# A two-layer graph network: which nodes are summed by counting and which by gathering, and how a float is split into three bf16 words

## The chip, the cores and the metric

The kernel runs on one core of one Trainium2 chip. The metric is the device time of one execution in microseconds (us), taken over several runs of the same program. One execution is also recorded by the profiler; its span runs from the first to the last instruction. The engines are called by the names of the profile: PE is TensorE (matrix products; PEld its weight loads), DVE is VectorE, ACT is ScalarE, POOL is GpSimd, SP is SyncE, which here only issues transfers.

## The reference

There are 12500 nodes with 256 features each and 200000 edges, sorted by destination. Destinations are skewed: `dst` is 12500 times the square of a uniform number, so low-numbered nodes receive many edges and high-numbered ones few. Two layers of mean aggregation are followed by a linear layer, a residual and a layer norm:

```python
def _sage_conv(x, src, dst, W_l, b_l, W_r):
    msgs = x[src]
    agg = jax.ops.segment_sum(msgs, dst, num_segments=N_NODES)
    deg = jax.ops.segment_sum(jnp.ones((src.shape[0],), x.dtype), dst, num_segments=N_NODES)
    mean = agg / jnp.maximum(deg, 1.0)[:, None]
    return mean @ W_l + b_l + x @ W_r

h = jax.nn.relu(_sage_conv(x, src, dst, W1_l, b1, W1_r))
h = jax.nn.relu(_sage_conv(h, src, dst, W2_l, b2, W2_r))
x = _layernorm(x + h @ W3 + b3, axis=-1)
```

All of it is float32.

## The kernel before

**Two ways to sum.** A segment sum is made in one of two ways. For the *cold* nodes (many nodes, few edges each) POOL gathers the rows of 128 source nodes at a time from DRAM with an indirect transfer (L251). A round is four such gathers. PE then multiplies the gathered rows by a 0/1 selection matrix (L263), which DVE makes by a comparison (L208), and the partial sums are placed by a second selection (L214, L279) and added by DVE into a ring of node blocks in SBUF (L293). There are four buffers `got`, so POOL can be some rounds ahead of PE.

For the *hot* nodes (few nodes, very many edges) nothing is gathered. Nodes are taken in groups of `DN` = 256. For a group the kernel first makes a matrix of counts: how many edges lead from each source node to each of the 256 nodes (`count`, L665). A tile of 128 edges is turned into 0/1 matrices by DVE (`pick` L680, `low` L684, `aft` L690), multiplied by PE into PSUM (L723, L727), and copied by ACT at a running offset into `counts` (L729). Then the sum is a dense product of counts and the whole node table (`product`, L642). The table is stored as three bf16 words per float, so that the product is exact: 98 blocks of source nodes times 3 words times 2 halves are 588 matmuls per group (L655), fed by 49 loads `rows` of 384 KB (L649) into four buffers.

**The words.** `split_rows` (L636) makes the three bf16 words of x in `x3_d` for layer 1, and `first_block` (L907) those of h in `h3_d` for layer 2. Both call `exact` (L629), in which ACT rounds the float to bf16, DVE subtracts it, ACT rounds the rest, and DVE subtracts again.

**Which groups are where.** `HG1` groups are summed by counts in layer 1 and `HG` in layer 2 (L102). The gathers of a layer begin behind its hot groups, at edge tile `lows[HG1]` or `lows[HG]`. Layer 1 runs in stages (`stages_1`, L807): in stage 0 group 0 is counted and x is split; in stage g group g is counted while the product of group g-1 runs, its degrees are summed (L744), and its counts are stored in DRAM (`stored`, L776). Two count buffers alternate. Groups 0 to 3 are stored; group 4 is kept and group 5 is counted already, so that layer 2 can begin with them. Layer 2 (`stages_2`, L819) takes groups 4, 5, 6, 0, 1, 2, 3 in this order: group 6 is counted during the product of group 5, and the stored counts of groups 0 to 3 are loaded again (`loaded`, L781) one stage ahead of their products.

**What orders the work.** PE and POOL keep the order in which the program is written; DVE, ACT and SP are ordered by the framework's scheduler. `layer` (L576) goes through the rounds of gathers. In each it issues the four gathers of the next round, the products of this round, pieces of finished node blocks (`first_block` or `last_block`), and as much dense and counting work as is due. What is due is a straight line: the planner's cost of all stages (`cost_of`) times the share of rounds done, reaching the whole eight rounds before the end (L615). Within a stage `mixed` (L762) takes its parts in proportion to their costs. So the counting and dense work is spread evenly over the rounds, and a change in the number of stages or rounds changes how much of it stands in each.

Before the gathers of layer 2 can start, all rows of h must have been written. The code that runs in case the edges do not fit the expected law (`by_sorting`) is not executed here.

Of the kernel before, what the change touches and what calls it, by code (L numbers as in the profile page):

```python
# [7 lines left out]
F32 = mybir.dt.float32  # L8
F16 = mybir.dt.float16
BF16 = mybir.dt.bfloat16  # L10
# [3 lines left out]
OP = mybir.AluOpType  # L14
# [9 lines left out]
P = 128  # L24
# [3 lines left out]
def kernel(tc, x, src, dst, w1l, b1, w1r, w2l, b2, w2r, w3, b3, out):  # L28

    args = (x, src, dst, w1l, b1, w1r, w2l, b2, w2r, w3, b3, out)
    flag = tc.nc.dram_tensor("unfit_d", (1, 1), I32).ap()
    by_runs(tc, *args, flag)
    with tc.tile_pool(name="flag", bufs=1) as pool:
        unfit_i = pool.tile([1, 1], I32, name="unfit_i")  # L40
        tc.nc.sync.dma_start(unfit_i, flag)
        unfit = tc.nc.values_load(
            unfit_i[0:1, 0:1], min_val=0, max_val=1,
            skip_runtime_bounds_check_because="it is clamped to 0..1 where it is made")
    with tc.If(unfit > 0):
        by_sorting(tc, *args)
# [3 lines left out]
def by_runs(  # L50
# [27 lines left out]
    nc = tc.nc  # L78
    N, D = x.shape
    E = src.shape[0]  # L80
    NB = -(-N // P)
# [15 lines left out]
    def at_most(t):  # L97
        return N * ((t + SLACK) / NT) ** 2 + 2

    HG1, HG, DN = 5, 7, 256  # L102
    lows = [max(t for t in range(0, NT, 2 * G) if t == 0 or at_most(t) < DN * g) for g in range(HG + 1)]
    highs = [min(t for t in range(0, NT, G) if at_least(t) >= DN * (g + 1)) for g in range(HG)]
    HT = highs[-1]
# [189 lines left out]
    with tc.tile_pool(name="setup", bufs=1) as su, \  # L295
# [172 lines left out]
        for g, (c0, c1) in enumerate(spans):  # L468
            n = c1 - c0
# [46 lines left out]
        for t in range(0, HT, 32):  # L516
            n = min(32, HT - t)
# [52 lines left out]
    work = ctx.enter_context(tc.tile_pool(name="work", bufs=2))  # L570
# [57 lines left out]

    def exact(t, s, rest):  # L629

        nc.scalar.copy(s[:, 0], t)
        nc.vector.tensor_tensor(rest, t, s[:, 0], op=OP.subtract)
        nc.scalar.copy(s[:, 1], rest)
        nc.vector.tensor_tensor(s[:, 2], rest, s[:, 1], op=OP.subtract)

    def split_rows(b):  # L636
        t = load_rows(x, N, b, "split_sb")
        s = work.tile([P, 3, D], BF16, name="parts")
        exact(t, s, t)
        nc.sync.dma_start(x3_d[:, b], s)  # L640

    def product(g, table3, c_sb):  # L642
# [116 lines left out]
    def counting(g):  # L759
        return sum(count_cost(t) for t in range(lows[g], highs[g]))  # L760
# [20 lines left out]
    def loaded(g, c_sb):  # L781
        for b0 in range(0, NB, 14):
            nc.sync.dma_start(c_sb[:, b0:b0 + 14, :DN], count_d[g, :, b0:b0 + 14])
            yield 0.5

    def dense(g, table3, c_sb, waiting, with_deg):
        for p in product(g, table3, c_sb):
            if isinstance(p, float):
                yield p
            else:  # L790
                d_sb = p
        if with_deg:
            yield from degrees(g, c_sb)
        for j in range(DN // P):
            waiting.append((g * (DN // P) + j, d_sb[:, :, j * P:(j + 1) * P]))

    def splits():
        for b in range(NB):
            split_rows(b)
            yield COST_SPLIT  # L800
# [1 line left out]
    D_1 = NB * COST_DENSE + DN // P * (NB // 14) * COST_DEGREES  # L802
    D_2 = NB * COST_DENSE
    MOVED = NB // 14 * 0.5
    assert NB % 14 == 0 and HG == HG1 + 2

    def stages_1(waiting):  # L807

# [9 lines left out]

    def stages_2(waiting):  # L819

        order = [HG1 - 1, HG1, HG1 + 1, *range(HG1 - 1)]
        for i, g in enumerate(order):
            parts = [(dense(g, h3_d, counts[(HG1 - 1 + i) % 2], waiting, False), D_2)]
            if 1 <= i < HG - 1:
                n = order[i + 1]
                to = counts[(HG1 + i) % 2]
                parts.append((count(n, to), counting(n)) if n > HG1 else (loaded(n, to), MOVED))
            yield parts
# [15 lines left out]
    def load_rows(table, n_rows, b, name, tag=None):  # L844
        t = work.tile([P, D], F32, name=name, tag=tag or name)
        n = min(P, n_rows - b * P)
        if n < P:
            nc.vector.memset(t, 0.0)
        nc.sync.dma_start(t[:n], table[b * P:b * P + n, :])
        return t  # L850
# [56 lines left out]
    def first_block(b, agg=None):  # L907
        x_sb = load_rows(x, N, b, "x_sb")
        of_ring = agg is None
        if of_ring:  # L910
            overlap(b, True)
            agg, deg_row = ring(b)
            nc.sync.dma_start(deg_d[b:b + 1], deg_row)
        yield True
        if of_ring:
            deg = work.tile([P, 1], F32, name="deg")
            with nc.allow_non_contiguous_dma(reason="a row becomes a column"):
                nc.sync.dma_start(deg, deg_d[b, :, None])
        x_t, copied = transposed(x_sb, turned(), "own_t")
        yield True  # L920
        if of_ring:
            nc.vector.tensor_scalar(deg, deg, 1.0, None, op0=OP.max)
            nc.vector.reciprocal(rdeg[:, b:b + 1], deg)
        h, own = sage(x_t, copied, b, agg, of_ring, w1l_sb, w1r_sb, biases[:, 0], "h")
        if of_ring:
            nc.scalar.copy(deg_row, zeros[0:1, 0])
        nc.sync.dma_start(h_d[b * P:(b + 1) * P, :], h)
        s = work.tile([P, 3, D], BF16, name="parts")
        exact(h, s, own)
        nc.sync.dma_start(h3_d[:, b], s)  # L930
        yield True
# [37 lines left out]
    block_pool = ctx.enter_context(tc.tile_pool(name="block_ps", bufs=2, space=PSUM))  # L969
    count_pool = ctx.enter_context(tc.tile_pool(name="count_ps", bufs=1, space=PSUM))  # L970
    layer(Gathers(h_d, True), last_block, 5, staged(stages_2), cost_of(stages_2))


# [377 lines left out]
```

## Time and profile before

| what | value |
|---|---|
| time, median of 3 runs | 2878.88 us (2876.56 to 2884.81) |
| the profiled execution | 2859.28 us, its span 2857.5 us |
| mean granted clock of TensorE | 0.918 |
| PE busy, matmul instructions | 2325.8 us (81%), 18268 |
| DVE busy | 1461.6 us (51%) |
| ACT busy | 1099.4 us (38%) |
| POOL busy, instructions | 2054.2 us (72%), 2074 |
| gathers in layer 1, in layer 2 | 1076 at 1031 ns, 988 at 954 ns |
| transfers | 676.49 MB, mean 237 GB/s |

Times are microseconds unless marked ns. A row of the groups gives line, engine and operation, output and inputs with their shapes, the number of instructions, the busy time and the mean ns of one, and the idle time before them with what ended it. "issue" is idle time in which the engine waited for nothing that the profile shows. A row of waits names the waiting group, what released it, the total, the number of times and the longest. A row by stretches gives the stretch, its length, the busy time of PE, PEld, DVE, ACT and POOL with instruction counts, the granted clock, the busy share of the transfer engines and GB/s. Matmuls overlap in PE, so the busy time of a group is less than its count times its mean.

### The profile page before, as it was taken

The numbers are of one execution on the slowest core, as the hardware profiler recorded it, in microseconds if no ns is written. First come the engines' busy times: TensorE is split into PE (matmuls) and PEld (weight loads), VectorE is DVE, ScalarE is ACT, GpSimd is POOL, SyncE is SP. The second block draws the span as 40 slices with busy tenths as digits, with TensorE's granted clock in tenths as the row PEclk, the third lists the DMA queues.
The fourth block names the chain that finished last, engine by engine and source line by source line (L and its number), as shares of the span: only waits on it lengthen the run. The fifth ranks groups of instructions, "written<-read, shape, count | busy, mean of one in ns | idle before, by whom it ended". The sixth has DMA issues, their size and how long they took to land.

```text
span 2857.5 us, 53445 instructions
## 1 busy us (share of the span) xinstructions
PE 2325.8 (81%) x18268; PEld 1607.4 (56%) x18268; DVE 1461.6 (51%) x4334; ACT 1099.4 (38%) x2270; POOL 2054.2 (72%) x2074
## 2 busy tenths in 40 slices
PE   3466675888988998999996678777889889999995
PEld 1122333565755666766664455555656667777773
DVE  6688774654555565565564124443324344444443
ACT  0422774654554564565563013333112122222222
POOL 5777775677777777777675777777777777777771
PEclk9876877997998999999997999999999999999998
DMA  4466679778878879877764777777989999888872
GB/s 124 135 180 179 190 210 300 248 225 257 267 224 254 291 219 297 262 215 228 247 212 132 229 244 231 222 225 226 294 285 306 295 301 309 283 264 270 271 248 70
DMA packets 420975, 676.49 MB, mean 237 GB/s; under 512 B 72420, under 2 KB 279386, under 8 KB 420698
## 3 DMA queue, kind: packets, MB, share of 16 engines
q1 hardware_dynamic: 316263, 400.60, 43.5%
q0 software_dynamic: 99072, 270.66, 31.3%
q8 instruction: 150, 2.46, 0.4%
q10 hardware_dynamic: 5362, 1.72, 0.3%
q14 instruction: 128, 1.04, 0.1%
HBM read 582.84 MB, written 89.92 MB: 235 GB/s over the span
## 4 chain that ended last, share of the span: by engine, by line
PE 45%; DMA 24%; POOL 11%; issue 8%; DVE 7%; ACT 4%; SPq 1%; DVEq 0%; ACTq 0%; POOLq 0%
PE dense_ps L655 17%; POOL got L251 11%; PE part_ps L263 6%; PE block_ps L878 5%; DMA got<-h_d,src_t 4%; DMA rows<-h_d 4%; PE block_ps L883 4%; PE count_ps L723 4%; DMA x_sb<-in_x_dram 4%; PE sum_ps L279 4%; DMA rows<-x_d 4%; DMA split_sb<-in_x_dram 3%; DMA got<-in_x_dram,src_t 2%; PE block_ps L950 2%; PE block_ps L855 2%
## 5 line engine op out<-in xcount | busy, mean ns | idle before, releaser
L251 POOL DMA_INDIRECT got<-in_x_dram,src_t x1076 | 1109.7, 1031 | 420.3 <-issue 282.7
L251 POOL DMA_INDIRECT got<-h_d,src_t x988 | 942.4, 954 | 329.4 <-issue 260.8
L655 PE MATMUL dense_ps<-counts,rows 128*128 128x256 bf16 x7056 | 958.4, 279 | 75.4 <-DMA rows<-h_d 41.1
L655 PEld LDWEIGHTS <-rows 128*128 128x128 bf16 x7056 | 674.2, 99 | 296.7 <-issue 81.4
L729 ACT CAST counts<-count_ps 128x686 f32 (+2 forms) x620 | 540.2, 872 | 237.8 <-PE count_ps L723 188.0
L263 PE MATMUL part_ps<-got,one 128*32 128x257 f32 (+1 forms) x4128 | 359.9, 422 | 181.9 <-DMA got<-h_d,src_t 106.1
L723 PE MATMUL count_ps<-pick,low 128*128 128x490 bf16 (+2 forms) x1052 | 321.1, 359 | 62.5 <-ACT counts L729 37.2
L680 DVE TENSOR_SCALAR pick<-steps,key_t 128x686 bf16<-128x686 f16 (+2 forms) x748 | 301.0, 414 | 120.9 <-PE count_ps L723 107.3
L208 DVE TENSOR_TENSOR one<-lo_t,lane_b 128x128 f32<-128x128 bf16 x516 | 148.1, 287 | 322.5 <-PE part_ps L263 318.8
L273 ACT COPY some<-part_ps 128x257 f32<-128x257 f32 (+1 forms) x361 | 134.5, 373 | 414.2 <-PE part_ps L263 413.1
L279 PE MATMUL sum_ps<-two,some 128*128 128x128 f32 x1444 | 240.9, 293 | 39.4 <-DVE own L890 38.6
L263 PEld LDWEIGHTS part_ps<-got,one 128*32 128x32 f32 x4128 | 87.2, 112 | 299.8 <-issue 237.9
L279 PEld LDWEIGHTS sum_ps<-two,some 128*128 128x128 f32 x1444 | 209.4, 205 | 55.3 <-DVE own L890 39.9
L293 DVE TENSOR_TENSOR sums<-sums,sum_ps 128x256 f32 x361 | 148.3, 411 | 145.8 <-PE sum_ps L279 113.2
L886 ACT COPY sums<-zero 128x256 f32<-128x256 f32 x172 | 69.3, 403 | 393.4 <-PE block_ps L883 391.8
L889 DVE TENSOR_TENSOR own<-block_ps,biases 128x256 f32<-128x256 f32 x196 | 82.6, 421 | 210.3 <-PE block_ps L883 209.9
L723 PEld LDWEIGHTS <-low 128*128 128x128 bf16 x1052 | 105.0, 101 | 140.0 <-DVE pick L680 33.6
L857 ACT COPY own_t<-block_ps 128x256 f32<-128x256 f32 x294 | 108.8, 372 | 125.6 <-PE block_ps L855 124.5
L684 DVE TENSOR_TENSOR low<-low_t,lane_b 128x512 bf16<-128x512 bf16 x187 | 127.7, 683 | 39.4 <-PE count_ps L727 39.0
L892 ACT ACTIVATE h<-own 128x256 f32<-128x256 f32 x196 | 81.7, 417 | 145.3 <-DVE own L890 145.0
L727 PE MATMUL count_ps<-aft,low 128*128 128x98 bf16 x614 | 133.3, 217 | 0.0
L878 PE MATMUL block_ps<-w1l_sb,sums 128*128 128x256 f32 x352 | 114.2, 453 | 12.5 <-DVE sums L293 6.0
(177 smaller groups left out, 2417.9 us busy)
## 6 DMA issues: line engine op xcount, KB each, us to landing
rows<-h_d SPq DMA_DIRECT2D x343, 384.0 KB
rows<-x_d SPq DMA_DIRECT2D x245, 384.0 KB
count_d<-counts SPq DMA_DIRECT2D x28, 896.0 KB
counts<-count_d SPq DMA_DIRECT2D x28, 896.0 KB
x_sb<-in_x_dram SPq DMA_DIRECT2D x194, 128.0 KB
x_d<-parts SPq DMA_DIRECT2D x98, 192.0 KB
h_d<-parts SPq DMA_DIRECT2D x98, 192.0 KB
got<-in_x_dram,src_t POOLq DMA_INDIRECT x1076
```

The costliest lines, as they stand in the source:

```text
L208: nc.vector.tensor_tensor(one, lo[:, a:a + n * (G - 1) + 1:n].unsqueeze(2).to_broadcast([P, G, W]), lane_b[:, :W].unsqueeze(1).to_broadcas ...
L251: rows = nc.gpsimd.indirect_dma_start(out=g[:, j, :D], out_offset=None, in_=self.table, in_offset=bass.IndirectOffsetOnAxis(ap=src_t[:, e: ...
L263: strip = nc.tensor.matmul(part_ps[j * W:(j + 1) * W, :width], lhsT=one[:, j], rhs=g[:, j, :width], start=r == 0, stop=r == n - 1)
L273: nc.scalar.copy(some[:, :width], part_ps[:, :width])
L279: nc.tensor.matmul(sum_ps[:, c], lhsT=some[:, c * P:(c + 1) * P], rhs=two, start=True, stop=True)
L293: nc.vector.tensor_add(own, own, sum_ps[:, :NC])
L655: nc.tensor.matmul(ps[:, c], lhsT=rows[:, b % 2, k, c * P:(c + 1) * P], rhs=c_sb[:, b, :DN], start=False, stop=b == NB - 1 and k == 2 and ...
L680: nc.vector.tensor_scalar(r[:, :w * NB], steps[:, :w * NB], key_t[g][:, t - lo_g:t - lo_g + 1], None, op0=OP.is_equal)
L723: nc.tensor.matmul(c[:, a * NB:b * NB], lhsT=s, rhs=r[:, a * NB:b * NB], start=True, stop=alone)
L727: nc.tensor.matmul(c[:, :NB], lhsT=before[0], rhs=before[1], start=False, stop=True)
L729: nc.scalar.copy(to[:, :, bass.ds(off_act.at(t), w)], c.rearrange("p (d s) -> p s d", s=NB))
L878: product = nc.tensor.matmul(ps[:, 0], lhsT=agg[:, c], rhs=wl[:, c], start=c == 0, stop=c == NC - 1)
```

## The change

`HG1` becomes 4 instead of 5. Group 4 (nodes 1024 to 1279) is no longer summed by counts in layer 1 but by gathers: the gathers of layer 1 begin at edge tile 432 instead of 488, in 283 rounds instead of 269. In layer 2 there are still seven groups. Layer 1 now has five stages instead of six and counts groups 0 to 4; groups 0 to 2 are stored and loaded. Layer 2 takes groups 3, 4, 5, 6, 0, 1, 2; group 5 is counted during the product of group 4, and group 6 during that of group 5.

`exact` no longer rounds. The first word is the upper half of the float's 32 bits, read in place as bf16; DVE subtracts it from the float, and subtracts the upper half of the rest from the rest, which is the third word. ACT copies the two upper halves into place. The rest needs its own tile in `split_rows`; it shares the two buffers of `own`.

```diff
-    HG1, HG, DN = 5, 7, 256
+    HG1, HG, DN = 4, 7, 256
...
     def exact(t, s, rest):
-        nc.scalar.copy(s[:, 0], t)
-        nc.vector.tensor_tensor(rest, t, s[:, 0], op=OP.subtract)
-        nc.scalar.copy(s[:, 1], rest)
-        nc.vector.tensor_tensor(s[:, 2], rest, s[:, 1], op=OP.subtract)
+        def upper(a):
+            return a.bitcast(BF16).rearrange("p (n h) -> p n h", h=2)[:, :, 1]
+
+        nc.vector.tensor_tensor(rest, t, upper(t), op=OP.subtract)
+        nc.vector.tensor_tensor(s[:, 2], rest, upper(rest), op=OP.subtract)
+        nc.scalar.copy(s[:, 0], upper(t))
+        nc.scalar.copy(s[:, 1], upper(rest))
 
     def split_rows(b):
         t = load_rows(x, N, b, "split_sb")
         s = work.tile([P, 3, D], BF16, name="parts")
-        exact(t, s, t)
+        exact(t, s, work.tile([P, D], F32, name="rest", tag="own"))
         nc.sync.dma_start(x3_d[:, b], s)
...
-    assert NB % 14 == 0 and HG == HG1 + 2
+    assert NB % 14 == 0 and HG > HG1
...
     def stages_2(waiting):
-        order = [HG1 - 1, HG1, HG1 + 1, *range(HG1 - 1)]
+        order = [*range(HG1 - 1, HG), *range(HG1 - 1)]
```

## The prediction

> **What bounds the kernel now.** I read the page first, then the list of who waits for whom on POOL, then the same by stretches of 100 us, last PE's waits. The page gives these totals (busy time, mean ns of one, then idle time before the group and what ended it):
>
> ```profile
> span 2857.5 us, 53445 instructions
> ...
> PE 2325.8 (81%) x18268; PEld 1607.4 (56%) x18268; DVE 1461.6 (51%) x4334; ACT 1099.4 (38%) x2270; POOL 2054.2 (72%) x2074
> ...
> L251 POOL DMA_INDIRECT got<-in_x_dram,src_t x1076 | 1109.7, 1031 | 420.3 <-issue 282.7
> L251 POOL DMA_INDIRECT got<-h_d,src_t x988 | 942.4, 954 | 329.4 <-issue 260.8
> L655 PE MATMUL dense_ps<-counts,rows 128*128 128x256 bf16 x7056 | 958.4, 279 | 75.4 <-DMA rows<-h_d 41.1
> ```
>
> By share PE looks like the limit and POOL like a rider. The reader is to see the idle time of the two L251 rows: nearly all of it is "issue". In the trace every gather is followed by 0.30 us in which POOL waits for nothing, so a gather of 0.95 us takes 1.25 us of POOL. Layer 2's gathers run from 1556.8 to 2804.6 us, 1247.8 us; 988 x (0.954 + 0.304) is 1243 us. **Layer 2 is POOL alone**, with about 5 us lost. Layer 1's gathers run from 24.8 to 1532.8 us, 1508 us: 1109.7 busy, 1075 x 0.304 = 327 between, and the remaining 71 us waits. Around these: 24.8 us of setup, 24.0 us between the layers (first gather of h waits for h_d) and 52.9 us of tail.
>
> Busy time by stretch (after the length: PE, PEld, DVE, ACT, POOL with instruction counts, then granted clock, DMA share, GB/s):
>
> ```profile
> 300.00:400.00 100.00, 71.44 (x413) 33.26 (x412) 80.92 (x243) 79.71 (x166) 77.67 (x74) 0.79 0.66 196
> 900.00:1000.00 100.00, 89.07 (x747) 63.84 (x747) 49.73 (x143) 49.05 (x91) 74.43 (x78) 0.97 0.93 304
> 1000.00:1100.00 100.00, 89.01 (x863) 64.08 (x856) 62.23 (x194) 58.14 (x112) 77.75 (x74) 0.98 0.75 229
> 1300.00:1400.00 100.00, 96.27 (x783) 70.40 (x782) 59.40 (x177) 56.62 (x106) 74.77 (x76) 1.00 0.81 256
> 1800.00:1900.00 100.00, 77.43 (x588) 52.08 (x588) 44.64 (x122) 39.24 (x63) 76.23 (x79) 0.93 0.72 218
> 2600.00:2700.00 100.00, 96.36 (x775) 74.30 (x774) 46.70 (x143) 26.08 (x73) 75.34 (x80) 1.00 0.84 271
> ```
>
> Divide POOL's busy time by its count: a gather takes 1.05 us where DVE is 81% busy (300), 0.95 at 50% (900), 1.05 at 62% (1000), 0.98 at 59% (1300), 0.965 at 45% (1800), 0.94 at 47% (2600). **A gather gets longer where DVE is dense.** Single ones show how: the gather at 1061.48 takes 3.2 us while DVE works without a gap. Against 0.945, layer 1's mean of 1031 ns is (1.031 - 0.945) x 1076 = 93 us, of which about 14 lie in the first 100 us.
>
> The 71 us of waits have one large place (waiter, releaser, us in total, times, longest):
>
> ```profile
> POOL got L251 <- PE count_ps L727: 19.0, 4, 18.1
> POOL got L251 <- issue: 14.3, 47, 0.3
> POOL got L251 <- PE part_ps L263: 7.9, 4, 3.5
> ```
>
> That is POOL from 400 to 500 us. About 25 us there and 13 in the next 100 us fall where the first stage (counting group 0, splitting x) goes over into the second. PE is behind, since ACT stands at L631 for x rows that are late among the 384 KB row loads and 896 KB count stores just begun. The rest: 9 us before 200 us, 7 around 750, 8 around 1450, small change.
>
> **The change, part by part.** *Groups.* Group 4 (nodes 1024 to 1279) goes to the gathers in layer 1: rounds 269 to 283, so 56 more gathers, and 186 to 193 sums. Gone from layer 1 are one dense product (588 x 0.136 = 80 us of PE, 49 row loads of 384 KB), 196 degree matmuls (7 us), 7 stores and 7 loads of 896 KB. Added beside the gathers: PE 14 x 0.70 + 7 x 0.67 = 14 us, 14 selections `one` (287 ns), 7 `two`, 7 copies of 373 ns, 7 additions of 411 ns, and for two blocks ring and degree handling with two small DMAs each. These hide below POOL; only the gathers are on its path: 56 x (0.945 + 0.304) = **+70 us**.
>
> *Counting of group 5* (72 tiles) moves into layer 2. PE pays (321.1 + 133.3)/614 = 0.74 us per tile, 53 us; ACT's copy about 1.01 us, 73 us; DVE 0.417 + (0.683 + 0.555)/4 = 0.73 us, 52 us. In layer 1 the paced costs (the program's own planner numbers) fall from 840.9 over 269 rounds to 713.9 over 283: 19% less counting, splitting and dense work per round. In layer 2 they rise from 529.4 to 579.0 over the same 247 rounds.
>
> *Layer 1's gain.* The first stage gets 26.6% of 283 rounds instead of 22.6% of 269, 75 instead of 61, for the same work. Counts and splits are about 240 us of DVE (236 tiles at 0.65, 98 splits at 0.84); DVE falls from about 80% to 75% there, and in later stages from 58% to 54%. From the rows above I take 0.04 us off a gather at 0.985 to 1.0 and 0.03 off the early ones, less for the longer first stage: mean 1.015 instead of 1.031. Waits: in the order of SP's queue as built, 22 of the 98 split loads stood behind the first count store before; now none does, so the 38 us at 400 to 530 should go, and PE's smaller load should take most of the rest. I leave 17 us. Layer 1: 1132 x (1.015 + 0.304) + 17 = **1510 us, +2**. Bounds: nothing recovered, 1132 x 1.335 + 71 = 1582 (+74); all of the excess gone but setup, 1414 + 14 + 9 = 1437 (-71).
>
> *Exact split.* Two DVE subtractions (0.42 us each) stay; two ACT casts (404 ns) now read every other 16-bit word. No row shows that read; I take 404 ns, with 300 to 800 as bounds, below POOL either way since ACT is 38% busy. The chain ACT-DVE-ACT-DVE becomes DVE-DVE with ACT beside it, some 0.8 us shorter per block. But the first to wait for the x rows is now DVE, with tests, `one` and sums queued behind; ACT's wait there was 87.0 us. Four buffered rounds of gathers (20 us) cover single waits of up to 6 us; uncovered it would be up to 87. The last blocks before layer 2 shorten by about 1 us. `rest` shares the two buffers of `own`: hidden at this pace.
>
> The Trainium skill ("SBUF — State Buffer", Who interferes with whom) weighs against this part's gain: a DVE instruction in a two-port mode holds the port pair shared with GpSimd, which then blocks for the whole instruction. By that rule the 72 tests (0.417 us) cost POOL up to 30 us in whichever layer they stand, and moving them saves nothing. The rows: counting in layer 2 lengthens gathers by 0.02 us (1800 against 2600) over some 240, about 5 us, while dense counting in layer 1 costs 0.05 and more. I follow the rows: **+5 us** in layer 2, 8 us less in layer 1 (inside the 1.015).
>
> *Layer 2's loss.* A dense stage with loads costs 69.6; of 239 paced rounds it got 31.4, now 28.7. Its 588 matmuls (79.9 us) are 2.54, then 2.78 us a round: +0.24. From 2500 to 2700 PE is busy 4.78 us of a 5.0 us round with POOL never held. 4.78 + 0.24 = 5.02: PE comes level with POOL in about the last 115 rounds. Before that counting is spread thinner than PE can carry (77% at 1800). Besides, PE already stands for rows:
>
> ```profile
> PE dense_ps L655 <- DMA rows<-h_d: 15.8, 5, 4.4
> ```
>
> This is 2057 to 2157 us, where PE had 16 us to spare; DMA share there was 0.90. The three stages with count loads now fall on rounds 125 to 211, where PE has nothing to spare, and rows come 9% denser. Uneven rounds cost some 0.1 us x 115 = 10 us, half of the row waits another 5: **+15 us**, between 0 (rows and PE still fit) and 40 (7 us per 100 over 430 us, and the 10).
>
> Sum: +2 + 5 + 15 - 1 = **+21 us**. The profiled execution took 2859.28 us, 1.8 us more than its span; it becomes about 2880. The median shown, 2878.88, is 19.6 us above that execution; I carry this over: **2900 us**.
>
> **Rivals.** *PE is the bound* (the page "Perfetto Trace Analysis", Identifying the Most-Contended Engine, would have us take the engine of highest occupancy, though it warns that busy time misleads for matmuls). PE loses 80 + 7 + its waits and pays 14; by that the time falls by 73 us to 2806. Against it: POOL's idle time is 0.30 us steps of issue. I give it 0.02, counted in the faster case below.
>
> *Faster: gathers shrink further.* One mechanism: the DVE trains that hold a gather thin out in layer 1, and its mean falls to 0.985, as at 1100 and 1300 today. Layer 1 is then 1132 x 1.289 + 17 = 1476, -32; with PE still fitting in layer 2 (+5) the time is 2852. It decides below a mean of 0.999 if layer 2 costs only the 5 us. For it: 0.954 at 900 with DVE at 50%; against it: the longer first stage is the dense one.
>
> *Slower: layer 1 recovers nothing.* DVE now stands for split rows, the mean stays 1.031, and 40 us of waits remain: 1551, +43; with layer 2's 20 the time is 2942.
>
> *Nothing moves:* the parts cancel within 0.3% (8.6 us), which is about what a measurement of this kernel can tell from no change.
>
> **Numbers.** The forecast's case 0.50 (2880 to 2925; slower in 0.43, within 0.3% in 0.07), faster 0.22 (0.20 clearly, 0.02 within), slower by no recovery 0.18, cancelling 0.10. So faster 0.20, same 0.19, slower 0.61. The range 2858 to 2940 leaves out most of the no-recovery case and the better part of a third of the faster one.
>
> **What would show it.** L251 in layer 1: 1132 gathers, mean near 1015 ns, non-issue waits below 25 us, none of 10 us at the first change of stage; it is wrong if the mean stays at 1030 or falls below 1000. DVE, not ACT, waiting for split_sb. In layer 2 988 gathers over 1265 to 1275 us, with POOL waiting for part_ps late; if they take 1250, PE still fitted. L655 with 6468 matmuls. A granted clock below 0.9 late in layer 2 would make PE the bound there and the loss larger.

## The result and the profile after

The changed kernel takes 2918.36 us (median of 4 runs, 2916.51 to 2928.63); the kernel before, in the same comparison, 2880.12 us (4 runs, 2876.56 to 2884.81). The ratio is 1.0139 (95% interval 1.0111 to 1.0167): slower by 38.2 us. The profiled execution of the changed kernel took 2916.51 us with a span of 2914.7 us and a granted clock of 0.906.

On some chips the kernel before takes 3356 to 3393 us instead of 2863 to 2887 us, and POOL is not the limit there; runs from those chips are compared with the kernel before on the same chip only, and are named below as runs on the other chips.

The page of the changed kernel, with the lines that answer to those shown of before:

```profile
span 2914.7 us, 52195 instructions
...
PE 2304.9 (79%) x17630; PEld 1572.2 (54%) x17630; DVE 1467.0 (50%) x4373; ACT 1104.2 (38%) x2282; POOL 2127.4 (73%) x2130
...
L251 POOL DMA_INDIRECT got<-in_x_dram,src_t x1132 | 1176.1, 1039 | 372.3 <-issue 301.6
L251 POOL DMA_INDIRECT got<-h_d,src_t x988 | 949.2, 961 | 356.6 <-issue 261.6
...
L659 PE MATMUL dense_ps<-counts,rows 128*128 128x256 bf16 x6468 | 872.0, 278 | 35.9 <-DMA rows<-h_d 28.0
```

588 matmuls of dense product are gone (7056 to 6468), 56 gathers have come (1076 to 1132), and most of POOL's idle time is still issue. Two numbers are to be read against the forecast: layer 1's mean gather is 1039 ns, longer than before (1031), and layer 2's gathers have 356.6 us of idle time around them instead of 329.4.

The list of waits of POOL (waiter, releaser, us in total, times, longest), changed kernel:

```profile
POOL got L251 <- issue: 563.3, 1847, 0.6
POOL got L251 <- PE part_ps L263: 52.8, 61, 6.1
POOL got L251 <- DMA h_d<-h: 25.1, 1, 25.1
```

The wait of 18.1 us for `count_ps` is gone, and no wait of 10 us is left except before the first gather and between the layers. The same list for the two stretches that matter gives, for `part_ps`, 3.7 us from 200 to 600 us (24.1 before) and, from 2250 us on, these totals (the kernel before, then the changed one):

```profile
POOL got L251 <- PE part_ps L263: 7.7, 11, 2.6
```

```profile
POOL got L251 <- PE part_ps L263: 37.1, 26, 6.1
```

The waits moved from the first stage of layer 1 to the end of layer 2.

Busy time by stretch (length, then PE, PEld, DVE, ACT, POOL with instruction counts, granted clock, DMA share, GB/s), changed kernel:

```profile
200.00:300.00 100.00, 55.39 (x299) 26.61 (x297) 61.46 (x174) 24.10 (x70) 79.28 (x69) 0.67 0.60 181
300.00:400.00 100.00, 56.05 (x300) 26.49 (x301) 71.07 (x185) 53.53 (x122) 78.95 (x66) 0.68 0.61 180
1800.00:1900.00 100.00, 78.26 (x602) 52.59 (x602) 47.53 (x127) 42.61 (x66) 76.23 (x79) 0.95 0.64 201
2300.00:2400.00 100.00, 85.37 (x704) 64.73 (x705) 35.32 (x109) 19.59 (x54) 70.47 (x75) 1.00 0.88 292
2500.00:2600.00 100.00, 91.99 (x724) 70.82 (x722) 41.75 (x127) 21.67 (x62) 67.70 (x72) 0.97 0.83 274
2600.00:2700.00 100.00, 97.58 (x809) 75.14 (x808) 43.64 (x133) 24.49 (x68) 75.89 (x80) 1.00 0.83 277
```

In the first stage a gather takes 79.28/69 = 1.15 and 78.95/66 = 1.20 us although DVE is less busy (61 and 71%) than it was (84% from 200 us, where a gather took 1.11, and 81% from 300 us, where it took 1.05). Late in layer 2, from 2300 to 2600 us, POOL does 72 to 75 gathers in 100 us instead of 79 or 80: it waits for PE. The kernel before in one of these stretches:

```profile
2500.00:2600.00 100.00, 95.25 (x791) 72.81 (x790) 44.73 (x138) 24.04 (x67) 74.88 (x80) 1.00 0.82 265
```

Where the time went, stretch by stretch of the two profiled executions (the end of one row is the start of the next):

| stretch | before, us | after, us | difference | forecast |
|---|---|---|---|---|
| to the first gather | 24.8 | 25.5 | +0.7 | 0 |
| gathers of layer 1 | 1508.0 | 1525.7 | +17.7 | +2 |
| between the layers | 24.0 | 25.1 | +1.1 | -1 |
| gathers of layer 2 | 1247.8 | 1280.6 | +32.8 | +20 |
| tail | 52.9 | 57.8 | +4.9 | 0 |
| span | 2857.5 | 2914.7 | +57.2 | +21 |

The profiled execution of before lay 19.6 us under its median when this was forecast; that of the changed kernel lies 1.9 us under its own. So the spans differ by 57.2 us and the medians by 38.2. The rows show where time is; the size of the change is the medians'. The row to doubt is that of layer 1. Three later profiles, under "What makes a gather longer", have the same layer 1 as the kernel before, in the same order of instructions, and take 1528, 1528 and 1523 us for it, with a mean gather of 1036 ns. They ran on another chip of the usual kind. Against those, layer 1 did not get longer, and the 33 us of layer 2 and 5 of the tail make up the 38.

### The profile page after: what moved, and what is told of

Its sections match the earlier page's. It is cut to its first block, busy times and chain, and to the rows that moved or that the text cites. A ratio compares the mean times of both kernels' runs of the same rounds, so it can differ in the third digit from the quotient of the medians.

```text
span 2914.7 us, 52195 instructions
## 1 busy us (share of the span) xinstructions
PE 2304.9 (79%) x17630; PEld 1572.2 (54%) x17630; DVE 1467.0 (50%) x4373; ACT 1104.2 (38%) x2282; POOL 2127.4 (73%) x2130
## 3 DMA queue, kind: packets, MB, share of 16 engines
q10 hardware_dynamic: 5390, 1.72, 0.3%
## 4 chain that ended last, share of the span: by engine, by line
PE 33%; POOL 20%; DMA 20%; issue 11%; DVE 2%; ACT 1%; DVEq 0%; SPq 0%; ACTq 0%; POOLq 0%
POOL got L251 20%; PE dense_ps L659 11%; DMA got<-in_x_dram,src_t 8%; DMA got<-h_d,src_t 5%; PE part_ps L263 5%; PE block_ps L882 4%; PE block_ps L887 4%; DMA rows<-h_d 3%; PE count_ps L727 3%; PE sum_ps L279 2%; DMA x_sb<-in_x_dram 2%; PE block_ps L954 2%; PE block_ps L859 1%; ACT counts L733 1%; DMA rows<-x_d 0%
## 5 line engine op out<-in xcount | busy, mean ns | idle before, releaser
L251 POOL DMA_INDIRECT got<-in_x_dram,src_t x1132 | 1176.1, 1039 | 372.3 <-issue 301.6
L251 POOL DMA_INDIRECT got<-h_d,src_t x988 | 949.2, 961 | 356.6 <-issue 261.6
L659 PE MATMUL dense_ps<-counts,rows 128*128 128x256 bf16 x6468 | 872.0, 278 | 35.9 <-DMA rows<-h_d 28.0
L659 PEld LDWEIGHTS <-rows 128*128 128x128 bf16 x6468 | 617.1, 99 | 237.4 <-issue 79.9
L263 PE MATMUL part_ps<-got,one 128*32 128x257 f32 (+1 forms) x4240 | 381.4, 433 | 363.6 <-DMA got<-in_x_dram,src_t 223.2
L684 DVE TENSOR_SCALAR pick<-steps,key_t 128x686 bf16<-128x686 f16 (+2 forms) x748 | 303.3, 414 | 130.8 <-PE count_ps L727 102.6
L263 PEld LDWEIGHTS part_ps<-got,one 128*32 128x32 f32 x4240 | 93.5, 113 | 484.5 <-issue 401.2
L208 DVE TENSOR_TENSOR one<-lo_t,lane_b 128x128 f32<-128x128 bf16 x530 | 152.2, 287 | 390.6 <-PE part_ps L263 387.3
L273 ACT COPY some<-part_ps 128x257 f32<-128x257 f32 (+1 forms) x368 | 136.8, 372 | 486.4 <-PE part_ps L263 484.3
L882 PE MATMUL block_ps<-w1l_sb,sums 128*128 128x256 f32 x360 | 129.8, 494 | 13.5 <-DVE sums L293 8.1
```

The lines of the kernel that those rows point to most:

```text
L208: nc.vector.tensor_tensor(one, lo[:, a:a + n * (G - 1) + 1:n].unsqueeze(2).to_broadcast([P, G, W]), lane_b[:, :W].unsqueeze(1).to_broadcas ...
L251: rows = nc.gpsimd.indirect_dma_start(out=g[:, j, :D], out_offset=None, in_=self.table, in_offset=bass.IndirectOffsetOnAxis(ap=src_t[:, e: ...
L263: strip = nc.tensor.matmul(part_ps[j * W:(j + 1) * W, :width], lhsT=one[:, j], rhs=g[:, j, :width], start=r == 0, stop=r == n - 1)
L273: nc.scalar.copy(some[:, :width], part_ps[:, :width])
L659: nc.tensor.matmul(ps[:, c], lhsT=rows[:, b % 2, k, c * P:(c + 1) * P], rhs=c_sb[:, b, :DN], start=False, stop=b == NB - 1 and k == 2 and ...
L684: nc.vector.tensor_scalar(r[:, :w * NB], steps[:, :w * NB], key_t[g][:, t - lo_g:t - lo_g + 1], None, op0=OP.is_equal)
```

## The experiments

### Each part alone

*Groups alone* is `HG1 = 4` with the old `exact`; *words alone* is `HG1 = 5` with the new one:

```diff
-    HG1, HG, DN = 5, 7, 256
+    HG1, HG, DN = 4, 7, 256
```

```diff
-        nc.scalar.copy(s[:, 0], t)
-        nc.vector.tensor_tensor(rest, t, s[:, 0], op=OP.subtract)
-        nc.scalar.copy(s[:, 1], rest)
-        nc.vector.tensor_tensor(s[:, 2], rest, s[:, 1], op=OP.subtract)
+        nc.vector.tensor_tensor(rest, t, upper(t), op=OP.subtract)
+        nc.vector.tensor_tensor(s[:, 2], rest, upper(rest), op=OP.subtract)
+        nc.scalar.copy(s[:, 0], upper(t))
+        nc.scalar.copy(s[:, 1], upper(rest))
```

They ran first on the other chips, three times each. What was expected of the first pair:

> Only the groups are changed (four and seven); the words are split as before, by rounding on ACT. Theory (the new split is what lengthens layer 1's gathers: its two DVE subtractions now stand back to back and hold a gather): the mean gather of layer 1 falls from the 1039 ns of the changed kernel to about 1015 ns, while the wait of POOL at the change from the first to the second stage comes back, 30 to 45 us in all of layer 1. Time near 2930 us. Rival (the first stage alone, longer and still dense with tests, lengthens them): the mean stays at 1035 to 1040 ns and the waits come on top, time near 2955 us. Layer 2 as in the changed kernel, about 1281 us of gathers.

> Only the split by halves of words is changed; five groups by counts in layer 1 as before. Theory: the stage-change wait of 38 us goes, layer 1's mean gather rises from 1031 to about 1050 ns (20 us), layer 2 keeps its 1248 us; time about 20 us below before, 2860 us. Rival (the new split doesn't lengthen gathers): mean 1030 ns, time about 40 us below before, 2840 us. If the wait does not go, time is above before.

Measured there: groups alone 1.0179 (1.0151 to 1.0207), in repeats 1.0168 (1.0101 to 1.0235) and 1.0142 (1.0083 to 1.0201); words alone 0.9932 (0.9899 to 0.9964), in repeats 0.9923 (0.9895 to 0.9951) and 0.9879 (0.9815 to 0.9943). The signs are clear, but the kernel before took 3356, 3393 and 3363 us on these chips, so the sizes could not be carried to the result. The changed kernel itself was run on the second of them:

> The changed kernel once more, beside the next three. If the gathers land as fast as in the first measurement: layer 1's mean gather 1035 to 1045 ns, waits of POOL in layer 1 below 15 us, layer 2's gathers over about 1280 us, ratio to before 1.010 to 1.020. If they land late, as in the runs above, where POOL waited for free buffers in every round: ratio 1.005 to 1.015.

It gave 1.0031 (1.0015 to 1.0046), below both ranges that were expected: the loss of 1.4% is nearly gone where POOL isn't the limit. So the parts were repeated on a chip where the kernel before takes its usual time (2887.15 us, 23 runs):

> Groups alone (four in layer 1, the old split of the words), on a chip where the kernel before takes about 2880 us and gathering sets the time. Theory (the new split lengthens layer 1's gathers by about 20 ns and ends the waits for split rows): mean gather near 1.019 us, waits at the first change of stage still there (30 to 50 us), layer 1's gathers 1132 x 1.323 + 40 = 1538 us, layer 2 as in the changed kernel (1280), so about 2925 to 2935 us, 1.6 to 2.0% above the kernel before. Rival (the split has no part in the gathers' length): mean 1.035 to 1.040 us, and about 2945 us or more. If the time is below 2910 the split, not the groups, made the changed kernel slower.

> Words alone (five groups in layer 1, the new split). Theory: mean gather in layer 1 near 1.055 us instead of 1.031 (1076 x 0.024 = 26 us lost), waits in layer 1 fall from 71 to below 30 us (40 us or more won), layer 2 unchanged at 1248, so 2860 to 2875 us, 0.2 to 0.7% below the kernel before. Rival (the waits come back elsewhere, since DVE stands for the rows of x): waits stay near 70 us, and the time is near 2905 us.

Measured: groups alone 2937.5 us, 1.0181 (1.0157 to 1.0206); words alone 2858.57 us, 0.9915 (0.9885 to 0.9945), the fastest version found. **The groups cost some 50 us, and the words win some 25 to 30.** The pages of the two, groups first:

```profile
L251 POOL DMA_INDIRECT got<-in_x_dram,src_t x1132 | 1167.1, 1031 | 393.4 <-issue 304.4
L251 POOL DMA_INDIRECT got<-h_d,src_t x988 | 949.4, 961 | 352.2 <-issue 260.7
```

```profile
L251 POOL DMA_INDIRECT got<-in_x_dram,src_t x1076 | 1134.4, 1054 | 374.0 <-issue 287.9
L251 POOL DMA_INDIRECT got<-h_d,src_t x988 | 942.9, 954 | 338.0 <-issue 259.3
```

And how they stand beside the profiles above. "Waits" in layer 1 is the gathers' whole time, less their busy time, less 0.304 us for each; the two means by stretch are of the gathers that begin in it, in ns:

| | before | groups | words | changed |
|---|---|---|---|---|
| gathers in layer 1 | 1076 | 1132 | 1076 | 1132 |
| their mean, ns | 1031 | 1031 | 1054 | 1039 |
| from 100 to 500 us | 1059 | 1067 | 1147 | 1117 |
| from 500 to 1500 us | 1011 | 1005 | 1010 | 999 |
| waits in layer 1, us | 71 | 27 | 24 | 6 |
| layer 1, us | 1508 | 1538 | 1485 | 1526 |
| layer 2, us | 1248 | 1279 | 1253 | 1281 |

Three things follow. First, **each part alone removes about 45 us of layer 1's waits**, and so largely the same ones: 71 to 27 with the groups, 71 to 24 with the words. Together they remove 65, not 91, and so the two ratios multiplied (1.0094) are less than that of the whole (1.0139). (In the three later profiles of the old layer 1 the waits are 82 to 87, so each part may remove some 55 to 60.) Second, the words pay for it in the gathers: with them, those of the first stage are 88 ns longer than before, and 50 ns longer than in groups alone. How firm the second figure is, the late-pace kernel below tells, whose layer 1 is the changed kernel's: 1079 there, only 12 more than groups alone, and a mean of 1032. On the other chips the sign is the same throughout: means of 1019, 1020 and 1020 with groups alone, 1035 to 1043 in four profiles with the changed layer 1, 1052 to 1058 with words alone. For words alone the length is 1076 x 0.023 = 25 us lost against 47 won, which gives the -23 us of layer 1. Third, **layer 2's loss belongs to the groups**: 31 us without the words, 6 with the words alone.

Of the expectations, the groups' ratio, layer 1's total and the words' mean held; the two times lie 1 to 3 us outside their ranges. For groups alone the mean was given as 1.019 and is 1.031 and the first-stage waits as 30 to 50 us and are 25 (23.7 for `part_ps` and 1.5 for `count_ps`): two misses that cancel. The 1.019 came from the other chips, so a gather's length doesn't carry over from there either.

The two copies of ACT, whose reading of every other 16-bit word no row of before showed, take 406 and 405 ns for x (L637, L638) where the casts took 404: as forecast.

### The pace of counting in layer 2

The changed kernel, with the counting of groups 5 and 6 entered in the planner at 0.74 of its cost. The same work is done; the stages behind the counting get more rounds.

```diff
+    LIGHT = 0.74
+
+    def lighter(costs):
+        for c in costs:
+            yield LIGHT * c
...
-                parts.append((count(n, to), counting(n)) if n > HG1 else (loaded(n, to), MOVED))
+                parts.append((lighter(count(n, to)), LIGHT * counting(n)) if n > HG1 else (loaded(n, to), MOVED))
```

> The changed kernel, but the planner's cost of counting in layer 2 is taken at 0.74, so that a dense stage with loads has again the 31.4 rounds that it had before, and the two counting stages 41.5 rounds each instead of 48. Theory (PE comes level with POOL in the late stages because they got fewer rounds): waits of POOL for part_ps from 2250 us on fall from about 35 to below 10 us, layer 2's gathers take about 1255 us instead of 1281, time about 2893 us. Rival (counting in layer 2 itself is too much for it, with its single PSUM buffer, or the transfers are): the waits move into the counting stages or stay, time 2915 to 2930 us.

> The changed kernel with the counting in layer 2 entered at 0.74 of its planned cost, so that the dense stages behind it get more rounds and start earlier. Theory (layer 2's loss is PE coming level with POOL in its last third): dense stages get about 31 rounds again, POOL's waits for part_ps after 2250 us fall from about 35 us to below 12, layer 2's gathers take 1255 to 1262 instead of 1281 us, and the time is about 2895 to 2900, 0.5 to 0.8% above the kernel before. Rival (the counting itself costs the 33 us, wherever it stands): layer 2 stays at 1275 to 1285, and the time at 2915 to 2920; the waits only move forward to the stages that count.

On the other chips it gave 1.0102 (1.0072 to 1.0132), and in repeats 1.0097 (1.0067 to 1.0128) and 1.0085 (1.0054 to 1.0115). On the second of these chips the changed kernel had 1.0031, so the lighter pace is worse there: a miss, left unexplained; POOL isn't what sets the time there. On the usual chip it gave 2897.09 us, 1.0044 (1.0025 to 1.0064). The stretches of this run, the same columns as above:

```profile
2300.00:2400.00 100.00, 92.47 (x754) 70.06 (x753) 43.19 (x131) 24.12 (x67) 73.68 (x79) 1.00 0.93 300
2400.00:2500.00 100.00, 90.72 (x731) 68.58 (x730) 40.24 (x125) 21.56 (x61) 75.93 (x80) 0.98 0.93 302
2500.00:2600.00 100.00, 91.57 (x731) 69.87 (x729) 44.57 (x138) 23.96 (x68) 71.76 (x77) 0.98 0.80 257
2700.00:2800.00 100.00, 96.77 (x795) 73.70 (x795) 45.93 (x142) 24.62 (x70) 75.64 (x81) 1.00 0.83 269
```

POOL is back at 77 to 81 gathers in 100 us. Layer 2's gathers take 1261 us instead of 1281, and POOL's waits for `part_ps` after 2250 us fall from 37.1 to 16.1 us:

```profile
POOL got L251 <- PE part_ps L263: 16.1, 15, 3.6
```

The same counting and the same products are done, so some 20 of the 33 us are a matter of where the work stands: PE level with POOL in the last third. Of the 13 us left, 6.5 are the gathers' own length (948.9 us busy against 942.4), put down to the counting beside them; groups alone, which count the same, have 949.4. The rival, that counting costs the 33 us wherever it stands, falls. The forecast waits below 12 us were too low.

### What makes a gather longer

Between 100 and 560 us, in five profiles of this kind (before, the changed kernel, groups, words, late pace), 104 gathers are longer than 1.45 us, and they hold 139 of the 222 us by which all gathers there exceed 0.945, the length of one that nothing holds up. One of them in the changed kernel (start us, duration us, engine, line):

```profile
366.88 0.67 DVE L688 TENSOR_TENSOR low<-low_t,lane_b 128x512 bf16<-128x512 bf16 x1
366.89 5.33 POOL L251 DMA_INDIRECT got<-in_x_dram,src_t  x1 [0.30 <-PE count_ps L727]
...
367.48 0.55 DVE L694 TENSOR_TENSOR aft<-after_t,steps 128x392 bf16<-128x392 f16 x1
...
367.95 0.41 DVE L635 TENSOR_TENSOR rest<-split_sb 128x256 f32<-128x256 f32 x1
...
368.55 0.40 DVE L636 TENSOR_TENSOR parts<-rest 128x256 bf16<-128x256 f32 x1
```

Between the lines shown and after them stand other work of DVE (tests at L684, selections at L208) and of other engines; DVE has no gap from before this gather's start to 371.5 us. But a run without a gap isn't enough: in the same profile a reduction of 10.65 us at 315.95 us (L739) lies over several gathers of 0.95 us. So the suspicion fell on the kinds of instruction, and three kernels put one kind each into layer 2 of the kernel before, at every fourth block of the dense products (175 times), written into a tile that nothing reads any more:

```diff
+    def burst(rows):
+        for _ in range(4):
+            nc.vector.tensor_scalar(idle[:, :882], steps[:, :882], lo2[:, 0:1], None, op0=OP.is_equal)
...
+            nc.vector.tensor_reduce(w1l_sb[:, 0, i:i + 1], w1r_sb.rearrange("p c f -> p (c f)"),
+                                    axis=mybir.AxisListType.X, op=OP.max)
...
+            nc.vector.tensor_tensor(idle[:, :512].bitcast(F32), w1r_sb[:, 0], w1r_sb[:, 1], op=OP.subtract)
...
+            if b % 4 == 0 and table3 is h3_d:
+                burst(rows)
```

> The kernel before, with four more tests (the instruction of the counting, 882 fp16 words to bf16) on DVE at every fourth block of each dense product of layer 2, into a weight tile that layer 2 no longer needs: 175 times about 1.9 us, some 330 us of DVE. Theory (tests of this kind hold a gather until DVE pauses): layer 2's mean gather rises from 954 to 1040 ns or more, and its gathers take 80 us longer at least. Rival (only DVE's share matters little, or the length has another cause): mean below 970 ns.

> The same with three reductions of 512 floats (0.6 us each) in the place of the four tests, some 310 us of DVE in the same places. Theory (it is the kind of instruction, not DVE's share): layer 2's mean gather stays at 950 to 965 ns, as the one reduction of 10.7 us in layer 1 left its gathers at 0.95 us. Rival (a dense DVE lengthens gathers whatever it does): mean 1000 ns or more, as in the run with tests.

> The same with four subtractions of two 256-float tiles in SBUF (0.42 us each, the instruction of the split) in the place of the tests, some 295 us of DVE. Theory (the two subtractions of the split hold gathers when they stand back to back): layer 2's mean gather rises to between 985 and 1040 ns. Rival (only the tests hold them, and the subtractions just fill the pauses between tests): below 970 ns in layer 2, where tests are few.

One run each, on a chip where the kernel before took 2863.1 us in one run. The rows, one kernel each (tests, reductions, subtractions): first the added work, then the gathers of layer 1, where nothing was added, and of layer 2.

```profile
L576 DVE TENSOR_SCALAR w1l_sb<-steps,lo 128x882 bf16<-128x882 f16 x700 | 343.9, 491 | 13.1
L251 POOL DMA_INDIRECT got<-in_x_dram,src_t x1076 | 1115.2, 1036 | 436.4 <-issue 281.4
L251 POOL DMA_INDIRECT got<-h_d,src_t x988 | 958.6, 970 | 340.9 <-issue 262.8
```

```profile
L576 DVE TENSOR_REDUCE w1l_sb<-w1r_sb 128x1 f32<-128x512 f32 x525 | 335.7, 675 | 0.0
L251 POOL DMA_INDIRECT got<-in_x_dram,src_t x1076 | 1114.4, 1036 | 435.5 <-issue 283.4
L251 POOL DMA_INDIRECT got<-h_d,src_t x988 | 945.8, 957 | 341.2 <-issue 261.0
```

```profile
L576 DVE TENSOR_TENSOR w1l_sb<-w1r_sb 128x256 f32<-128x256 f32 x700 | 295.3, 422 | 13.1
L251 POOL DMA_INDIRECT got<-in_x_dram,src_t x1076 | 1114.2, 1036 | 430.9 <-issue 282.4
L251 POOL DMA_INDIRECT got<-h_d,src_t x988 | 965.7, 977 | 337.6 <-issue 262.7
```

Each adds some 300 to 340 us to DVE, which is then 65 to 83% busy from 1600 to 2200 us. The gathers of layer 2 grow from 954 ns to 957 with reductions, 970 with tests and 977 with subtractions; in the six profiles with five groups in layer 1 and nothing added they have 950 to 955, so the reductions' 3 ns are hardly clear of that spread. The theories for tests (1040 ns or more) and subtractions (985 or more) expected far more. So **DVE's busy share is not what lengthens a gather here; the kind of instruction is**. Spread over what was added, a subtraction of two SBUF tiles costs the gathers 23.3/700 = 33 ns, a test 16.2/700 = 23 ns, a reduction 3.4/525 = 6 ns. The Trainium skill ("SBUF — State Buffer", Who interferes with whom) holds that a reduction never contends with GpSimd, which the row bears out nearly. It says that a DVE instruction with two SBUF inputs contends with a GpSimd instruction that reads SBUF; the gather takes its row numbers from `src_t`, a tile in SBUF, and the 977 against 954 ns fits that. It reports that `tensor_tensor` did not stall DMA, and infers that this is because making descriptors needs the write interface of the shared ports; the row shows a gather lengthened, though no run here tells which of its accesses is held up. It also has a two-port instruction block GpSimd for its whole length; if the tests ran in such a mode, which no run here shows, 23 ns of each 491 is far less.

The times of the three, 2908.8, 2895.89 and 2907.86 us, rose by 33 to 46 us, more than the 3 to 23 us of the gathers. In layer 2 POOL also waited longer for `part_ps` (24.2, 21.3 and 18.8 us instead of 9.6). But 15 to 20 us of the rise stand in layer 1 (1528, 1528 and 1523 us instead of 1508), where nothing was added: its waits are 86, 87 and 82 us instead of 71, and its gathers 1036 ns instead of 1031. That is how far executions of the same code differ here, and the one profile of the kernel before is at the short end. The times are therefore not read as the price of the gathers.

What this leaves open is the size in layer 1. Added alone, no kind makes a gather of layer 2 longer than 1.72 us; in the first stage some take 3 to 5. In the 104 long gathers above, `low` and `aft` make up 29% of the DVE time beside them (16% beside the others), and the two subtractions of the new split 24% (22%), while those of the old split make up 13% (24%). This points to the bf16 comparisons of `low` and `aft`, and to mixed runs of which the new subtractions have become a part, now that no ACT copy stands between them. It is a count of what coincides, not a test.

### One hop back

To see whether it matters that the two subtractions stand back to back, the second was made to read the word that ACT has copied, so that one trip to ACT lies between them:

```diff
         nc.vector.tensor_tensor(rest, t, upper(t), op=OP.subtract)
-        nc.vector.tensor_tensor(s[:, 2], rest, upper(rest), op=OP.subtract)
         nc.scalar.copy(s[:, 0], upper(t))
         nc.scalar.copy(s[:, 1], upper(rest))
+        nc.vector.tensor_tensor(s[:, 2], rest, s[:, 1], op=OP.subtract)
```

> The changed kernel, but the second subtraction reads the word that ACT has copied, so that the two DVE subtractions are parted by a hop to ACT. Theory (two subtractions back to back lengthen the gathers): layer 1's mean falls from 1039 to about 1020 ns, time about 20 us below the changed kernel, 2898 us, with no stage-change wait as long as the split loads stay ahead of the count stores. Rival (the length comes from the tests of counting, not from the pair): mean within 5 ns of 1039, time 2913 to 2923 us.

> Five groups as before, words split by halves, but the second subtraction reads the word that ACT copied, so that the two subtractions are parted. Theory: the stage-change wait is gone as with the new split, and layer 1's mean gather is 7 to 15 ns shorter than with the pair back to back, about 1045 ns: ratio 0.988 to 0.995, the fastest of the four. Rival (parting them does nothing): ratio as that of the words alone.

Both ran on the other chips. On top of the changed kernel the ratio is 1.0035 (1.0016 to 1.0053), with a mean gather in layer 1 of 1032 ns, against 1042 for the changed kernel on another chip of that kind and 1035 for the late-pace kernel, with the same layer 1, on the same chip; on top of words alone it is 0.9898 (0.9844 to 0.9953), against 0.9879 for words alone on the same chip, with 1034 against 1052 ns:

```profile
L251 POOL DMA_INDIRECT got<-in_x_dram,src_t x1076 | 1112.2, 1034 | 639.0 <-issue 264.8
```

On top of words alone the gathers get 18 ns shorter on one chip, which is more than words alone differed by between three chips (1052 to 1058). So it matters for the gathers how the two subtractions stand, as far as one profile of each shows. On top of the changed kernel it is 2 ns on the same chip and 10 between two chips, within the spread of that layer 1 (1035 to 1043), so nothing is shown there. The time didn't follow, since POOL doesn't set it on these chips. It wasn't tried on a usual one.

## Why the prediction was right or wrong

**What bounds the kernel: right.** Layer 2 is POOL alone at 1.25 us a gather, and taking 588 matmuls and 49 row loads out of layer 1 won nothing. The rival of PE as the bound fell.

**Groups, +70 us: right in size.** The 56 gathers at the measured 1.031 + 0.304 us are 75 us. Less the 45 us of waits that groups alone remove in layer 1, plus 31 in layer 2 and 7 in the tail, that makes 68, and the profiled spans differ by 67 (2924.6 against 2857.5). The medians differ by 50.

**Waits of layer 1: right, and better than forecast.** From 71 to 6 us, not 17, with none of 10 us at the first change of stage; DVE now stands for `split_sb` (16.0 us from 200 to 600 us), as was said, and the buffered gathers cover it. Either edit by itself takes them to 27 or 24.

**The gather's length in layer 1: wrong, and the step that failed.** It read "A gather gets longer where DVE is dense" and took 0.03 to 0.04 us off for a thinner DVE, to a mean of 1.015. It measured 1.039: 0.024 x 1132 = 27 us, less the 11 us better waits, is the 16 us by which layer 1 missed. Part of the step held: from 500 to 1500 us the gathers fell from 1011 to 999 ns. In the first stage they rose from 1059 to 1117, at a smaller DVE share. In the rows of before, tests, comparisons and share rise together; the reductions show that share alone does next to nothing. Of the 27 us, 18 stand in groups alone too, whose mean stays at 1031: less counting and dense work in each round did not shorten the gathers there. Why fewer tests and comparisons a round did not is open; on the other chips groups alone have 1019 and 1020, near the forecast. The other 9 us came with the words: that their two subtractions "stay" was costed at nothing, though they were put back to back. The late-pace run, whose layer 1 has the same code, has 1079 ns from 100 to 500 us and a mean of 1032, so 8 of the 27 us lie within what two executions differ by.

As a change, the forecast of +2 for layer 1 may have come near, but by luck. Against the three later profiles of the old layer 1 (1036 ns, 82 to 87 us of waits) it is -3 to +3: the gathers got no shorter, and the waits fell by 76 us or more instead of 54.

**Layer 2, +5 and +15: right mechanism, too small.** The gathers' own price was 6.8 us against the 5. PE coming level with POOL late was sized at 15, with bounds of 0 and 40, and measured 26: of the sum's terms the second that was too small. The counting that moved was undersized too: 0.74 us of PE a tile is the mean over all tiles, but those counted in layer 2 are the widest, 882 words, and take (26.3 + 22.9 + 14.2)/68 = 0.93 us there in the kernel before, so 67 us for 72 tiles and not 53. The row waits that were to add 5 are there: from 2250 us on PE waits 28.0 us for `rows` instead of 15.7. The late-pace run shows the mechanism. The clock is not the cause: late in layer 2 it is 0.97 to 1.00, before the change 0.98 to 1.00. The skill's rule of a full block, by which the 72 tests would have cost up to 30 us in either layer, was rightly put below the rows.

**Tail and setup: not forecast.** +4.9 and +0.7 us. Words alone has a tail of 56.6, groups alone 59.8 us; what sets it was not looked into.

**Carrying over the 19.6 us: wrong.** It assumed that every profiled execution lies as far under its median as that of before. Those of the later kernels on usual chips lie 2 to 11 us under theirs. By luck this error made up for half of the sum's: 36 us too little in the sum, 18 too much here, and 2900 stood against 2918.

**The rivals.** Layer 1 recovering nothing (2942) was right on the length of the gathers and wrong on the waits; the time ended between it and the forecast. Shrinking further and cancelling are out.

## What to carry to other kernels

Where POOL's gathers set the time, count what stands beside them by kind of DVE instruction, not by DVE's busy share: here reductions were nearly free beside a gather, two-input subtractions and tests were not, and parting two subtractions shortened the gathers in one pair of profiles. When two edits remove the same wait, add their gains only once; here each alone removed 45 us of waits and both 65. Before a row is compared with one profile, see how far executions of the same code lie apart: here layer 1 had 1508 to 1528 us. Work moved to a stage with room still raises the density of every later stage if a planner spreads a fixed number of rounds over it, and the price is paid where PE has no room left; the remedy was to enter the moved work below its cost.

## What the runs showed of the hardware that was not expected

Some chips run this program 17% slower. On them the kernel before took 3356 to 3393 us; the granted clock in the profiles there is 0.85 to 0.88, and POOL, with the same gather length, is 62% busy. The chain that ended last in the changed kernel on such a chip, and the list of POOL's waits:

```profile
PE 50%; another core or an unknown queue 11%; issue 9%; ACT 4%; DVE 3%; DMA 3%; POOL 2%; SPq 0%; DVEq 0%; ACTq 0%; POOLq 0%
```

```profile
POOL got L251 <- PE part_ps L263: 202.3, 80, 10.5
POOL got L251 <- remote: 196.8, 105, 3.8
```

The chain goes through PE, where on the usual chip it ran 20% through POOL, and some 200 us of POOL's waits are put down to a releaser that the trace doesn't hold. The dense matmul is hardly slower (286 ns against 278). ACT has the same: its copy `some` waits 484.3 us for PE's `part_ps` on the usual chip, and there 130.7 for it and 292.8 for this releaser. That would fit products that end later than their records say, which nothing here shows. What differs between the chips was not found.

A subtraction of two SBUF tiles lengthens the gathers beside it more (33 ns each) than a test that takes longer (23 ns), as the rows above show.
